# A transformer block on one core: the MLP's first layer by two levels of seven products instead of one

## The chip, the core and the metric

The kernel runs on one core of a Trainium2 chip. Its engines are TensorE (PE: matmuls, and their weight loads PEld), VectorE (DVE), ScalarE (ACT), GpSimd (POOL) and SyncE (SP, which here only starts transfers); each works through its own queue in order, and semaphores tie them together. The metric is device time in microseconds (us) of one execution.

## The reference

The input x has 2 sequences of 2048 tokens with 512 features; all is float32. With D = 512, 16 heads and a hidden width of 2048:

```python
mod = silu(condition) @ Wada + bada
sh_a, sc_a, gt_a, sh_m, sc_m, gt_m = split(mod, 6, axis=1)
xm = layernorm(x, g1, be1) * (1.0 + sc_a[:, None, :]) + sh_a[:, None, :]
x = x + gt_a[:, None, :] * causal_attention(xm, Wqkv, Wproj, bproj)
xm = layernorm(x, g2, be2) * (1.0 + sc_m[:, None, :]) + sh_m[:, None, :]
h = gelu(xm @ W1 + b1)                          # W1: 512 x 2048
x = x + gt_m[:, None, :] * (h @ W2 + b2)        # W2: 2048 x 512
```

## The kernel before

The first two thirds of the time go to modulation, the q, k, v products and the causal attention of the two sequences (`Row(0)`, `Row(1)`), each with its output projection (`project_phase`). The last third, from 1605 us on in the profiled execution, is the MLP. This is where the change is.

**Seven products.** A product of two 2x2 block matrices needs eight block products; with sums of blocks taken first, seven do (Winograd's form of Strassen's method). The code names them A11, S1, S2, S3, S4, A12, A22, and `seven` runs them over three accumulators in PSUM: `ps_a` takes A11, S2, S3 and A22 one on top of the other, `ps_b` takes S1 and S4, `ps_c` takes A12. After each product the accumulator's present value is taken out: `first` keeps it in a spare tile `c`, `last` adds an earlier `c` and yields a quarter of the result. So a later product on the same accumulator must wait until the earlier value has been read. The sums of the weights' blocks are made ahead, in the class `Quarters`, on GpSimd (L913) during the q, k, v stages, and kept in DRAM (`w1d`, `w2d`, L902). The sums of the tokens' blocks are made on VectorE (`difference`, L1239).

**The MLP's loop.** It takes `NM` = 4 pairs of groups of 512 tokens, 1024 tokens at a time. For each pair:

- First layer (`Hidden.block`, L1462, once for each of `HF` = 8 columns of weight blocks): one level of seven products over (two halves of the 512 features) x (two halves of the hidden width) x (two groups of tokens). A product is `HK` = 2 matmuls of 128x128 weights with 512 tokens. ScalarE copies three values out (L1483), VectorE adds (`combine`, L1318), and ScalarE applies the bias and gelu (L1492) as it writes the hidden values `h`.
- Second layer (`Hidden.outer`, L1502, called by `tail`, once for each of the seven outer names): two levels. The outer level splits the hidden width, the output features and the groups of tokens; inside each of its seven, `seven` runs again on halves of those. A product is `C` = 4 matmuls with 256 tokens. The token sums that this needs are a list of tasks in an order written out by hand in `Hidden.__init__`: `inner(n)` gives the four inner sums of the outer name n, `first_sums`, `difference_of` give the outer sums T1 to T4. `hid.pop` runs the next task, normally one after each product; `need` runs tasks at once, in order, until the one that the next product needs is done. Some tasks are already run in the first layer (`among` in the main loop, up to six).

In the second layer of a pair the next pair is normalised and transposed (`normed`, `ln_t`); in the first layer the pair before is transposed back, added to the residual and stored (`rows_out`, after products of the second and third block).

**Order.** Matmuls and the operations wrapped in `act(...)` keep the order of the program on their engine. Weights come in through SP's queue (`load_w1`, `load_w2`) into three rotating tiles `w7`; a load is issued when the tile that it overwrites has been used.

Of the kernel before, what the change touches and what calls it, by code (L numbers as in the profile page):

```python
# [8 lines left out]
F32 = mybir.dt.float32  # L9
F32R = mybir.dt.float32r  # L10
# [17 lines left out]
def dit_block_kernel(  # L28
# [99 lines left out]
    def picks():  # L128
# [56 lines left out]
    w1d = [  # L185
        dram.tile([P, 7, C // 2, P], F32, tag=f"w1d{f}", name=f"w1d{f}")
        for f in range(FC // 2)
    ]
    w2d = [
        dram.tile([P, C, 7, P], F32, tag=f"w2d{n}", name=f"w2d{n}")  # L190
        for n in range(7)
# [38 lines left out]
    def transposed(pool_, psum, xts, n0, mv, rstd, a, c, b, dst, xns=None):  # L230
# [8 lines left out]
        for t, xt in enumerate(xts):  # L239
            if by_act:  # L240
                continue
            xn = pool_.tile([P, D], F32, tag="xn", name="xn", bufs=3)
            n = n0 + t
            nc.vector.tensor_scalar(
                xn, xt, mv[:, n, 0:1], rstd[:, n : n + 1], ALU.subtract, ALU.mult
            )
            xns.append(xn)
# [512 lines left out]
    class Qkv:  # L760
# [41 lines left out]
        def group(self, g, hp, between, among):  # L802
# [6 lines left out]
            for f in range(C):  # L809
                for which in range(2):  # L810
# [8 lines left out]
                    hl = hp.tile([P, 2, MT], F32R, tag="hl", name="hl", bufs=4 - b)  # L819
# [69 lines left out]
    class Quarters:  # L889
# [25 lines left out]
        def step(self):  # L915

            self.store()
            f, self.at = self.at, self.at + 1
            if f >= FC // 2 + C:
                return  # L920
            if not self.rooms:
                self.rooms = self.more_rooms()
            w = self.rooms.pop(0)
            base = ((A11, 0, 0), (A12, 0, 1), (A21, 1, 0), (A22, 1, 1))
            if f < FC // 2:
                w = w[:, :piece].rearrange("p (n c d) -> p n c d", n=7, d=P)
                for n, i, k in base:
                    at = (f + i * FC // 2) * P
                    nc.gpsimd.dma_start(
                        w[:, n],  # L930
                        w1_v[:, k * C // 2 : (k + 1) * C // 2, at : at + P],
                    )
                self.sums(lambda n: w[:, n])
                self.to = [(w1d[f], w)]
                return
            r = f - FC // 2
            w = w.rearrange("p (n k d) -> p n k d", n=7, k=7)
            for n, i, k in base:
                for n2, i2 in ((A11, 0), (A21, 1)):
                    at = (2 * i + i2) * P  # L940
                    k0 = 2 * k * C + r
                    nc.gpsimd.dma_start(
                        w[:, n, n2 : n2 + 3 : 2],
                        w2_v[:, k0 : k0 + C + 1 : C, at : at + P],
                    )
            self.sums(lambda n: w[:, n, A11 : A22 + 1])
            self.sums(lambda n: w[:, :, n])
            self.to = [(w2d[n][:, r], w[:, n]) for n in range(7)]
            self.store()
# [208 lines left out]
    with pool("qkv1") as qp, pool("ps_qkv1", bufs=6, space=PSUM) as ps_mm:  # L1158
# [18 lines left out]
        def also(g, n):  # L1177
            k = NG * g + n // 4
            if n % 4 == 1 and (k < 2 or k % 2 == 0):
                quarters.step()  # L1180

        with pool("hl1") as hp:
            def rooms():

                w = hp.tile([P, 49 * P], F32, tag="w7", name="w7")
                if quarters.at > FC // 2:
                    return [w]
                return [w[:, k * piece : (k + 1) * piece] for k in range(2)]

            quarters.more_rooms = rooms  # L1190
            qkv.run(hp, also)
            assert quarters.at >= FC // 2 + C
            quarters.store()
# [8 lines left out]
    with ExitStack() as mlp:  # L1202
# [4 lines left out]
        OUTER = (A11, S1, A12, S2, S3, A22, S4)  # L1207
        half_t = MT // 2
# [14 lines left out]
        def normed(m, n, xts):  # L1223

            xns = []
            for t, xt in enumerate(xts):
                k = 2 * m * MTT + 2 * n + t
                xn = wp.tile([P, D], F32, tag="xn", name="xn", bufs=3)
# [23 lines left out]
        def load_w1(f):  # L1252
            w = wp.tile([P, C * C * P], F32, tag="w7", name="w7", bufs=3)
            w = w[:, :piece].rearrange("p (n k d) -> p n k d", n=7, k=HK)
            nc.sync.dma_start(w, w1d[f])
            return w

        def load_w2(n, part):
            k = C - part
            w = wp.tile([P, C * C * P], F32, tag="w7", name="w7", bufs=3)  # L1260
            w = w[:, : C * k * P].rearrange("p (r k d) -> p r k d", k=k, d=P)
            nc.sync.dma_start(w, w2d[n][:, :, C * part : C * part + k])
            return w

        loads = []
        for _ in range(NM):
            loads += [lambda f=f: load_w1(f) for f in range(HF)]
            loads += [lambda n=n, k=k: load_w2(n, k) for n in OUTER for k in range(2)]
        w7 = []

        def next_weights():
            if loads:
                w7.append(loads.pop(0)())
# [32 lines left out]
        for _ in range(3):  # L1306
            next_weights()
# [6 lines left out]
        ]  # L1314
        Y = [mp.tile([P, 2, MT], F32, tag=f"y{n}", name=f"y{n}", bufs=1) for n in range(4)]
# [7 lines left out]
        def seven(product, w, first, last, among):  # L1323

            def bank(name):
                return ps_mm.tile([P, MT], F32, tag="mm", name=name)[:, :w]

            a, b = bank("ps_a"), bank("ps_b")
            product(a, A11, True)
            c11 = first(a, 0, 0)
            among(0)
            product(b, S1, True)  # L1340
            c22 = first(b, 1, 1)
            among(1)
            product(a, S2, False)
            c12 = first(a, 0, 1)
            among(2)
            product(b, S4, False)
            last(b, 0, 1, c12)
            among(3)
            product(a, S3, False)
            last(a, 1, 1, c22)  # L1350
            among(4)
            c = bank("ps_c")
            product(c, A12, True)
            last(c, 0, 0, c11)
            among(5)
            product(a, A22, False)
            last(a, 1, 0, None)
            among(6)

        class Hidden:  # L1360
# [3 lines left out]
            def __init__(self):  # L1364
# [7 lines left out]
                self.todo, self.made, self.at = [], set(), 0  # L1372
# [35 lines left out]

                first_sums(0)
                difference_of("T3", b12, b22, b12, 0, (0,))  # L1410
                inner(A11, (1,))
                inner(S1, (1,))
                inner(A11, (2, 3, 4))
                first_sums(1)
                inner(S1, (2, 3, 4))
                inner(A12)
# [45 lines left out]
            def block(self, f, among):  # L1462

                w = w7.pop(0)
# [6 lines left out]
                }  # L1471

                def product(ps, n, new):
                    for k in range(HK):
                        mm(
                            ps, w[:, n, k, :], ops[n][:, k],
                            start=new and k == 0, stop=k == HK - 1,
                            skip_group_check=not new,
                        )

                def first(ps, half, g):
                    c = spare(MT)
                    act(nc.scalar.copy(c, ps))  # L1483
                    return c

                def last(ps, half, g, c):
                    d = self.part(half, g, f)
                    if c is not None:
                        combine(d, c, ps)
                        ps = d  # L1490
                    act(
                        nc.scalar.activation(  # L1492
                            d, ps, AF.Gelu, bias=col(r_b1 + half * HF + f, 1)
                        )
                    )

                seven(product, MT, first, last, among)
                next_weights()

            def outer(self, n, dst, base, among, each=None):  # L1500

                w = []  # L1502
# [12 lines left out]
                def product(ps, k, new):  # L1515
# [4 lines left out]
                    if k in (A11, S3):  # L1520
                        w.append(w7.pop(0))
                    at = k - C * (len(w) - 1)
                    y = ops[k]()
                    for r in range(C):
                        mm(
                            ps, w[-1][:, r, at, :], y[:, r],
# [5 lines left out]
                    if k in (S4, A22):  # L1532
                        next_weights()
# [23 lines left out]
                seven(product, half_t, first, last, among)  # L1557
# [11 lines left out]
        def tail(m, hid, among, each):  # L1569
# [13 lines left out]
            for n, dst, base in (  # L1583
# [9 lines left out]
                def then(k):  # L1593
                    if k in (1, 3) and later:
                        later.pop(0)()
                    hid.pop()
                    among(n, k)
# [45 lines left out]
        ready = False  # L1643
        for m in range(NM):
            hid = Hidden()
            for f in range(HF):

                def among(k):
                    if f >= C and k in (2, 5):
                        if len(hid.made) < 6:  # L1650
                            hid.pop()
                    if ready and f in (1, 2) and k == 6:
                        rows_out(m - 1, f - 1, res, [(0, C)], True)

                hid.block(f, among)
                if ready and f < 2:
                    res = residual(m - 1, f, "xr")
# [81 lines left out]
```

## Time and profile before

| what | value |
|---|---|
| time, median of 3 runs | 2367.77 us (2367.48 to 2368.69) |
| profiled execution: time / span | 2366.88 us / 2365.2 us |
| TensorE clock granted | 1.00 |
| busy: PE, DVE, POOL, ACT | 2336.9, 1397.6, 1079.2, 924.1 us |
| one first layer (pair 0: 1605.21 to 1701.35 us) | 8 blocks x 7 products |
| one second layer (pair 0: 1701.35 to 1789.46 us) | 7 x 7 products and 4 groups of transposes |

The profile's times count from the span's start. A matmul of float32 appears in the records as two instructions: the first layer's 448 matmuls with 512 tokens are 896 rows, the second layer's 784 with 256 tokens are 1568 rows. A row's duration contains the time in the array's pipeline, which overlaps the next matmul; what a product takes of TensorE's time is the distance from its start to the next one's. Operation names are given as output<-inputs, with the tiles' names.

### The profile page before, as it was taken

To read this page: it belongs to the slowest core of one execution; us is meant where nothing else is said; L and a number is where in the kernel's file an instruction comes from. 1 tells how busy PE (TensorE), PEld (TensorE's weight loads), DVE (VectorE), ACT (ScalarE), POOL (GpSimd) and SP (SyncE) were. 2 spreads that over 40 slices of the span, in tenths; PEclk is the share of its full clock that TensorE was granted. 3 is DMA by queue.
4 is the path that set the end of the run, shared out by engine and by line. 5 is a ranking of instruction groups with operands and counts; after the bars stand their busy time and mean duration, and the time that the engine had idled before them with its cause. 6 is when DMAs were issued, how large, how long until landed. Compare 5 with 4: busy or idle time off the path is not lost.

```text
span 2365.2 us, 32348 instructions
## 1 busy us (share of the span) xinstructions
PE 2336.9 (99%) x11469; PEld 1294.6 (55%) x11469; DVE 1397.6 (59%) x2868; ACT 924.1 (39%) x1736; POOL 1079.2 (46%) x1219
## 2 busy tenths in 40 slices
PE   8999999999999999999999999999999999999998
PEld 4455555555544445555555555444585486487477
DVE  3466666767656636576666766553483374365356
ACT  2113555555555012155555555613322332332321
POOL 1052997978793646379887997460000000000000
PEclk9999999999999999999999999999999999999999
DMA  7577215151223788650513214272254254353433
GB/s 258 188 249 195 49 28 118 27 117 46 83 106 132 255 259 259 220 113 24 117 46 85 59 31 144 78 252 100 98 170 146 94 179 139 119 166 132 135 124 129
DMA packets 134106, 311.49 MB, mean 132 GB/s; under 512 B 14208, under 2 KB 29100, under 8 KB 129080
## 3 DMA queue, kind: packets, MB, share of 16 engines
q1 hardware_dynamic: 126096, 277.13, 38.9%
q0 software_dynamic: 7472, 31.75, 3.7%
q8 instruction: 90, 1.47, 0.3%
q14 instruction: 72, 0.59, 0.1%
q10 hardware_dynamic: 376, 0.55, 0.1%
HBM read 229.95 MB, written 87.29 MB: 134 GB/s over the span
## 4 chain that ended last, share of the span: by engine, by line
PE 96%; DVE 2%; POOL 1%; issue 0%; DMA 0%; ACT 0%; SPq 0%; POOLq 0%; ACTq 0%; DVEq 0%
PE st L203 20%; PE ps_a L203 17%; PE o L203 11%; PE s L203 10%; PE ps_qk L203 9%; PE ps_b L203 9%; PE ps_v L203 5%; PE ps_o L203 5%; PE ps_c L203 4%; PE sm L203 4%; PE ps_xt L211 1%; POOL ee L614 1%; PE ps_o L211 1%; DVE mx L461 0%; DVE junk L456 0%
## 5 line engine op out<-in xcount | busy, mean ns | idle before, releaser
L586 ACT ACTIVATE e<-st 128x512 f32<-128x512 f32 (+1 forms) x1152 | 574.6, 578 | 428.1 <-PE st L203 361.6
L614 POOL TENSOR_TENSOR ee<-ee,e 128x512 f32<-128x512 f32 x424 | 529.2, 1289 | 4.4 <-ACT e L586 4.0
L461 DVE TENSOR_REDUCE mx<-s 128x1 f32<-128x512 f32 x604 | 407.9, 688 | 204.5 <-PE s L203 203.1
L203 PE MATMUL s<-kst,qst 128*128 128x512 f32 (+3 forms) x1032 | 463.7, 451 | 5.7 <-DVE mx L461 2.9
L203 PE MATMUL st<-qst,kst 128*128 128x512 f32 (+3 forms) x1280 | 409.4, 387 | 0.0
L203 PE MATMUL ps_a<-sum,w 128*128 128x256 f32 (+1 forms) x1088 | 346.6, 454 | 0.0
L203 PE MATMUL o<-e,vv 128*32 128x512 f32 (+3 forms) x2560 | 300.5, 538 | 2.0 <-POOL e L592 2.0
L456 DVE CUSTOM_DVE_ANT_0 junk<-s,causal 128x512 bf16<-128x512 f32 (+3 forms) x428 | 209.3, 489 | 135.5 <-PE s L203 127.6
L203 PEld LDWEIGHTS s<-kst,qst 128*128 128x128 f32 x1032 | 194.4, 189 | 155.7 <-DVE mx L461 55.6
L203 PEld LDWEIGHTS st<-qst,kst 128*128 128x128 f32 x1280 | 227.3, 188 | 94.2 <-issue 62.2
L203 PEld LDWEIGHTS ps_a<-sum,w 128*128 128x128 f32 x1088 | 206.3, 190 | 109.8 <-issue 91.4
L614 POOL TENSOR_TENSOR ee<-e 128x512 f32<-128x512 f32 x168 | 210.4, 1285 | 101.4 <-ACT e L586 101.0
L203 PE MATMUL ps_qk<-xmT,wqkv 128*128 128x512 f32 x512 | 239.0, 594 | 1.8 <-DVE xmT L263 1.8
L592 POOL TENSOR_SCALAR_AFFINE_SELECT e<-e 128x128 f32<-128x128 f32 (+1 forms) x384 | 122.4, 357 | 135.0 <-ACT e L586 132.3
L203 PE MATMUL st<-fold,sel 32*128 32x512 f32 (+1 forms) x1152 | 149.1, 481 | 0.9 <-ACT vv L843 0.5
L203 PEld LDWEIGHTS ps_qk<-xmT,wqkv 128*128 128x128 f32 x512 | 93.9, 190 | 97.0 <-issue 90.4
L1318 DVE TENSOR_TENSOR h<-c,ps_b 128x512 f32<-128x512 f32 x32 | 22.0, 687 | 202.4 <-PE ps_b L203 202.4
L203 PEld LDWEIGHTS st<-fold,sel 32*128 32x128 f32 x1152 | 59.3, 181 | 144.8 <-ACT e L586 86.6
L203 PE MATMUL ps_v<-wqkv,xmT 128*128 128x512 f32 x256 | 122.3, 594 | 0.0
L203 PE MATMUL ps_b<-sum,w 128*128 128x256 f32 (+1 forms) x384 | 120.6, 450 | 0.0
L203 PEld LDWEIGHTS o<-e,vv 128*32 128x32 f32 x2560 | 61.1, 108 | 102.0 <-issue 81.0
L1492 ACT ACTIVATE h<-h,cols 128x512 f32<-128x512 f32 x96 | 69.2, 721 | 118.6 <-DVE h L1318 118.6
(155 smaller groups left out, 2601.3 us busy)
## 6 DMA issues: line engine op xcount, KB each, us to landing
qst<-q SPq DMA_DIRECT2D x128, 256.0 KB
w<-w1d SPq DMA_DIRECT2D x32, 896.0 KB
w<-w2d SPq DMA_DIRECT2D x28, 1024.0 KB
kst<-k SPq DMA_DIRECT2D x24, 1024.0 KB
w<-w2d SPq DMA_DIRECT2D x28, 768.0 KB
q<-hl SPq DMA_DIRECT2D x32, 512.0 KB
k<-hl SPq DMA_DIRECT2D x32, 512.0 KB
w2d<-w POOLq DMA_DIRECT2D x28, 448.0 KB, 6.5
```

The costliest lines, as they stand in the source:

```text
L203: return tc.keep_in_program_order(nc.tensor.matmul(*args, **kw))
L211: return tc.keep_in_program_order(nc.tensor.transpose(dst, src, ident[:n, :n]))
L456: nc.vector.tensor_tensor_reduce(junk[:, :w], s[:, :w], causal[:, QB - w :], 1.0, MASKED, ALU.add, ALU.max, m,)
L461: nc.vector.tensor_reduce(m, s[:, :w], axis=AX.X, op=ALU.max)
L586: act(nc.scalar.activation(e[:, :w], sts[h][:, :w], AF.Exp))
L592: nc.gpsimd.affine_select(d, d, pattern=[[0, len(tiles)], [1, P]], compare_op=ALU.is_ge, fill=0.0, base=0, channel_multiplier=-1,)
L614: act(engine.tensor_tensor(dst, x, y, ALU.add))
L1318: act(nc.vector.tensor_tensor(dst, x, y, ALU.add))
L1492: nc.scalar.activation(d, ps, AF.Gelu, bias=col(r_b1 + half * HF + f, 1))
```

## The change

The first layer goes to two levels as well: `first_layer` takes the place of `block`. The outer level is the same split as before; inside each of its seven steps (`one_outer`) the seven products run again, over halves of (256 features) x (1024 hidden columns) x (512 tokens). A product is 4 matmuls of 128x128 weights with 256 tokens, and each accumulator is two PSUM banks (a pair of 128-column blocks in each). Each step gives a quarter matrix of hidden values; since the outer level has to add these too, they stay in the tiles of `h`, and the outer sums are made there in place: in each step after the first two, an earlier matrix (`base`) is added to the values taken out, on VectorE, or, for two of them, on GpSimd after ScalarE's copy; two further sums (`adds`, four operations each) follow the steps S2 and S3. Gelu becomes a pass of its own, in place, from a list `later`, two operations after each product. After the first step the inner order begins with S1 rather than A11.

`Quarters` now makes only the outer sums of both weights. The inner sums are made in the MLP's first pair by GpSimd (`Weights.add`: four operations a step, one after each product from the fourth on) in the tile that holds the step's weights, and stored from there to DRAM (`w1e`, `w2e`); the later pairs load them ready. The weights of a step (14 KB a partition) have one of two rooms.

The order of the tasks in `Hidden` changes (`inner(A11)` comes first, T3's first half later), and four rather than six tasks are run ahead in the first layer. Outside the MLP, `transposed` normalises in place (`xn = xt`), and the tile `hl` has four buffers in the second sequence instead of three.

```diff
-            xn = pool_.tile([P, D], F32, tag="xn", name="xn", bufs=3)
+            xn = xt
...
-                    hl = hp.tile([P, 2, MT], F32R, tag="hl", name="hl", bufs=4 - b)
+                    hl = hp.tile([P, 2, MT], F32R, tag="hl", name="hl", bufs=4)
...
+        class Weights:
+            def load(self, at, part):
...
+                m, layer, n = order[at]
+                room = rooms[at % 2]
+                if m:
+                    k = slice(0, 3) if part == 0 else slice(3, 7)
+                    nc.sync.dma_start(room[:, k], (w1e if layer == 1 else w2e)[n][:, k])
+                elif part:
+                    src = (w1d if layer == 1 else w2d)[:, n]
+                    nc.sync.dma_start(
+                        room[:, 2:6], src.rearrange("p k (i f) d -> p (k i) (f d)", i=2)
+                    )
+                    self.adding.append((at, 0))
+            def add(self):
...
+                    nc.gpsimd.tensor_tensor(
+                        room[:, slot[d]], room[:, slot[x]], room[:, slot[y]], op
+                    )
...
+                if step < 3:
+                    self.adding.insert(0, (at, step + 1))
+                else:
+                    nc.gpsimd.dma_start((w1e if layer == 1 else w2e)[n], room)
+            def used(self, k):
+                if k == 2:
+                    self.load(self.at + 2, 0)
+                elif k == 6:
+                    self.load(self.at + 2, 1)
+                if k >= 3:
+                    while self.adding and self.adding[0][0] == self.at + 1:
+                        before = len(self.adding)
+                        self.add()
+                        if k < 6 or len(self.adding) < before:
+                            break
...
+            if lead == A11:
+                a = bank("ps_a")
+                c11 = one(a, A11, 0, True, 0, 0, False)
+                b = bank("ps_b")
+                c22 = one(b, S1, 1, True, 1, 1, False)
+            else:
+                b = bank("ps_b")
+                c22 = one(b, S1, 0, True, 1, 1, False)
+                a = bank("ps_a")
+                c11 = one(a, A11, 1, True, 0, 0, False)
+            c12 = one(a, S2, 2, False, 0, 1, False)
+            one(b, S4, 3, False, 0, 1, c12)
+            one(a, S3, 4, False, 1, 1, c22)
             c = bank("ps_c")
+            one(c, A12, 5, True, 0, 0, c11)
+            one(a, A22, 6, False, 1, 0)
...
+                inner(A11)
                 first_sums(0)
-                difference_of("T3", b12, b22, b12, 0, (0,))
-                inner(A11, (1,))
                 inner(S1, (1,))
-                inner(A11, (2, 3, 4))
                 first_sums(1)
                 inner(S1, (2, 3, 4))
+                difference_of("T3", b12, b22, b12, 0, (0,))
                 inner(A12)
...
+                    def first(ps, i, t):
+                        cs = []
+                        for pair in range(2):
+                            c = spare(MT).rearrange("p (r t) -> p r t", r=2)
+                            if base is None:
+                                act(nc.scalar.copy(c, ps[pair]))
+                            elif (i, t) == (0, 1):
+                                combine(c, piece_of(base, i, t, pair), ps[pair])
+                            else:
+                                act(nc.scalar.copy(c, ps[pair]))
+                                act(
+                                    nc.gpsimd.tensor_tensor(
+                                        c, c, piece_of(base, i, t, pair), ALU.add
+                                    )
+                                )
+                            cs.append(c)
+                        return cs
...
+                    def then(k):
+                        self.gelu()
+                        for _ in range(2):
+                            if adds:
+                                adds.pop(0)()
+                        if todo and todo[0][0] <= at + 1:
+                            inner_x()
+                        elif at >= 5 and len(self.made) < 4:
+                            self.pop()
+                        among(at, k)
...
+                for at, (n, dst, base) in enumerate((
+                    (A11, u, None),
+                    (S1, c22, None),
+                    (A12, c11, u),
+                    (S2, u, u),
+                    (S3, u, u),
+                    (S4, c12, c12),
+                    (A22, u, u),
+                )):
+                    one_outer(at, n, dst, base)
+                    if n in (S2, S3):
+                        d = c12 if n == S2 else c22
+                        for i in range(2):
+                            for pair in range(2):
+                                adds.append(
+                                    lambda d=d, i=i, pair=pair: combine(
+                                        rows4(*d, i, pair), rows4(*u, i, pair),
+                                        rows4(*c22, i, pair),
+                                    )
+                                )
```

## The prediction

> **What bounds the kernel now.** I read the page's busy line and its 40 slices first.
>
> ```profile
> PE 2336.9 (99%) x11469; PEld 1294.6 (55%) x11469; DVE 1397.6 (59%) x2868; ACT 924.1 (39%) x1736; POOL 1079.2 (46%) x1219
> PE   8999999999999999999999999999999999999998
> PEclk9999999999999999999999999999999999999999
> DVE  3466666767656636576666766553483374365356
> POOL 1052997978793646379887997460000000000000
> ```
>
> TensorE is the bound everywhere, at full clock. The MLP is the last 13 slices: POOL is idle there, DVE 30 to 80% busy. So fewer matmuls are time won, one for one, until another engine makes TensorE wait; the question is only where that happens. TensorE's timeline gives the products' pitch in both layers (columns: start, us, engine, line, operation, output<-inputs, count).
>
> ```profile
> 1605.21 1.88 PE L203 MATMUL ps_a<-xm,w 128*128 128x512 f32 x4
> 1606.93 1.88 PE L203 MATMUL ps_b<-sum,w 128*128 128x512 f32 x4
> ...
> 1699.63 1.88 PE L203 MATMUL ps_a<-sum,w 128*128 128x512 f32 x4
> 1701.35 1.89 PE L203 MATMUL ps_a<-h,w 128*128 128x256 f32 x8
> 1703.07 1.89 PE L203 MATMUL ps_b<-sum,w 128*128 128x256 f32 x8
> ...
> 1789.46 1.88 PE L203 MATMUL ps_a<-xm,w 128*128 128x512 f32 x4
> ```
>
> First layer of pair 0: 1605.21 to 1701.35, 56 products, 96.15/56 = 1.717 us each. A second-layer product, four matmuls with 256 tokens, is what the first layer will now have: 1701.35 to 1789.46 less 3.5 for groups of transposes gives 84.6/49 = 1.727 us. ScalarE's timeline shows when a result can be read, VectorE's what its sums cost.
>
> ```profile
> 1791.37 0.59 ACT L1483 COPY c<-ps_a 128x512 f32<-128x512 f32 x1 [0.45 <-PE ps_a L203]
> ```
>
> The product begun at 1789.46 hands over at 1791.17 and is read at 1791.37: 0.20 us after the next begins.
>
> ```profile
> 1765.48 0.42 DVE L1318 TENSOR_TENSOR y<-y,ps_a 128x256 f32<-128x256 f32 x1 [0.17 <-PE ps_a L203]
> 1765.82 1.22 DVE L1239 TENSOR_TENSOR sum<-h 128x1024 f32<-128x1024 f32 x1
> 1766.96 1.22 DVE L1318 TENSOR_TENSOR y<-y,y 128x1024 f32<-128x1024 f32 x1
> 1768.10 0.41 DVE L1318 TENSOR_TENSOR c<-y,ps_a 128x256 f32<-128x256 f32 x1
> ```
>
> A sum of 1024 elements takes 1.14 us from start to start, one of 256 about 0.34; 512 elements out of PSUM 0.69 (0.64 apart, by the group h<-c,ps_b). While these run, POOL is idle. What DVE and POOL do to each other shows only in the attention, on both timelines:
>
> ```profile
> 725.69 3.58 DVE L614 TENSOR_TENSOR ee<-e 128x512 f32<-128x512 f32 x4
> ...
> 725.86 1.67 POOL L434 TENSOR_TENSOR kst<-kst,bgate 128x512 f32<-128x512 f32 x1 [16.81 <-DVE bgate L424]
> ```
>
> Four DVE sums take 2.48 us in a row elsewhere (at 729.91), here 3.58: during one POOL sum, DVE lost 1.10 us. By the answer for source line 614, such a DVE sum takes 682 ns in the median and 1766 at most. [...]
>
> **The matmuls.** A pair's first layer goes from 56 x 1.717 to 49 x 1.727 us: 96.15 to 84.6, so 11.5 saved, four pairs: **-46.1**. [...]
>
> In what follows a step is one of the seven outer ones (7 x 1.727 = 12.1 us), S its start.
>
> **Starts.** The first inner sums of a layer now need two sums in a row on VectorE, behind the last results of the second layer, or in pair 0 behind the normalising. Pair 0: five sums of 0.34 are 1.7, with 0.06 to resume, 1.8; later pairs some 0.5, as A11's token sums go behind two evictions. **+3.3** (0 to 8).
>
> **Gelu.** A product fills its accumulator's two banks one after the other, so a half can be read while the other is made: S1's halves at S + 1.06 and 1.93 (0.86 and 1.73, and 0.20). In step S2 ScalarE's queue holds S1's copies, the first two gelus, then A11's copies: 1.93 + 0.59 = 2.52, gelus (0.70 apart, L1492) to 3.92, A11's first copy to 4.51, and the S2 product on the same bank at 4.57 rather than 3.45: 1.1 a pair, and one table load of 1.28 (the row of ACT_TABLE_LOAD): **+5.7** (0 to 12). Behind it on ScalarE wait only further copies. Gelus of later steps lie in the shadow of the next term.
>
> **Adds against POOL.** After steps S2 and S3, DVE gets four adds of 1.14 in the first two products of the next step, and two inner sums of 0.34, from S + 0.9, when the last results are out. Alone these end at 6.1. The S3 product, due at 6.9, needs ps_a's S2 value read, which stands behind them: 6.1 + 0.64 + 0.06 = 6.8, no wait. But in the same stretch POOL has its four adds on `c` (ready behind ScalarE's copies of S1 and A11 at 1.65, 2.5, 3.4 and 4.3), and each costs DVE 1.1: 10.3 rather than 6.1, and S3's product runs at 11.0, 4.1 late. Behind DVE's eviction wait the accumulator, and TensorE's whole queue. Eight such steps at 4.2 are 33.6, with about 3 more in pair 0, where POOL also sums weights: **+36.6**. Bounds: nothing (the two dodge each other), and 8 x 4 x 1.77 = 57 if every POOL add costs DVE a full blocked row. I take near one loss per POOL add, as the row above has it.
>
> **Step A22.** Before it DVE has, in S4, four adds, four inner sums, about ten evictions and three second-layer tasks, more than 12.1 us. What is left over makes A11's and S3's products wait some 1.6 each: 4 x 1.6 = **+6.4** (0 to 13).
>
> **Second layer.** Only four tasks are ahead instead of six, so the fourth sums of S2 and A22 are run by `need` behind the S1 product of their own step; before, they were done a step earlier. Each is 1.22 on DVE plus what stands ahead of it: S2's product waits 1.75, A22's 2.4, 4.1 a pair: **+16.4** (0 to 25; 0 if DVE runs ahead).
>
> **Weights in pair 0.** POOL's four sums a step block second-layer tasks as above: **+4** (0 to 10). The transfers I take as hidden. A room turns round in two steps, 24.2 us: load 5.3 + sums 5.1 + store 9.2 (1792 KB by the row below, 4.6 per 896 KB) = 19.6.
>
> ```profile
> w1d<-w POOLq DMA_DIRECT2D x8, 896.0 KB, 4.6
> ```
>
> Load and store are 2.88 MB in 12.1 us, 238 GB/s; the slices reach 259. By the slow row of that view (wqkv through POOL's queue, 1024 KB in 11.6) it would be 11.6 + 5.1 + 20.3 = 37, up to 6.4 late a step, and 90 us over 14 steps. That is the range's far end; I take the near row, the same kind of store to DRAM.
>
> **Nothing for.** `xn` in place: x's buffer comes free after TensorE's transposes instead of DVE, covered by the five projections (some 17 us) before it is reloaded; a full miss would cost one load of 256 KB. `hl` with four buffers and the smaller `Quarters` lie under the q, k, v matmuls, where the POOL slices leave gaps; +-3. Rows_out loses DVE room: +0.3.
>
> **Sum.** 3.3 + 5.7 + 36.6 + 6.4 + 16.4 + 4 = 72.4 lost, 46.1 won: +26.3. The profiled execution of 2366.9 becomes 2393.2; the median of the runs was 0.9 above that execution: **2394**.
>
> **The rivals.** *The other side, the adds dodge:* DVE and POOL run beside each other, or POOL's adds fall into DVE's gaps. The two terms on blocking (36.6 and 4) go, the others stay at 31.8, and the time is 2367.8 - 14.3 = 2353. For it: POOL's adds are only 5 of a step's 12.1 us, and DVE's evictions out of PSUM leave holes. Against it: the 1.10 us above, and that adds and `c` are both released in the first half of a step. It decides where blocking costs under 14.3 us, 1.8 at each of the eight steps. *Pair 0 short of weights:* the slow DMA row holds in part; +26 (up to +90) on the forecast, 2420. For it, POOL's queue carries 1.8 MB a step, ahead of which it must finish its sums; against it, the row of 4.6. *Only the matmuls count:* all waits hidden by slack, 2321; against it, TensorE has now only 12.1 us a step and DVE more than that in S4. *No change:* the terms balance within 5 us.
>
> **How the numbers follow.** Forecast 0.60, the adds dodge 0.22 (2340 to 2362), weights late 0.10, matmuls alone 0.04, no change 0.04. A measurement here tells 0.2%, 4.7 us, from nothing. The forecast's low edge and the balance give 0.07 within it; 0.25 below, 0.68 above. The likeliest's own range is 2378 to 2412 (term four between 20 and 55); to hold 8 in 10 it must take in most of the dodge case and some of the late weights: 2350 to 2416.
>
> **What would show it.** First-layer products at 1.727 where nothing waits; TensorE idle before the S3 product of steps S3 and S4, about 4 us each, released by DVE on ps_a; DVE's 1024-element adds at 2.2 rather than 1.2 us while POOL works; waits of 1.7 to 2.4 on the task sums in the second layer's S2 and A22; in pair 0, no waits on `w`. Wrong if those adds keep 1.2 us (then the dodge), or if TensorE's long waits are on a DMA or POOL and end with pair 0 (late weights).

## The result, and the profile after

The changed kernel takes 2405.47 us (median of 4 runs, 2401.53 to 2407.41) against 2367.62 for the kernel before in the same comparison: ratio 1.0157, interval 1.0139 to 1.0175. The profiled execution took 2403.96 us with a span of 2402.2, 37.0 more than before.

The page of the kernel after: busy line, and the slices of the four engines and the clock.

```profile
PE 2320.7 (97%) x12141; PEld 1433.0 (60%) x12141; DVE 1632.3 (68%) x3164; ACT 937.1 (39%) x1784; POOL 1264.5 (53%) x1349
PE   8999999999999999999999999998899899899998
DVE  3466666766757536667666666657896876877787
POOL 1062898978774561089787979356662400310310
PEclk9999999999999999999999999999899999999999
```

TensorE is busy 16 us less and the kernel is 37 us longer. In the MLP, from slice 27 on, POOL is no longer idle, and TensorE has holes in the slices of three of the four first layers (the 8s in slices 28, 29, 32 and 35; in the fourth the slices stay at 90% or more). The waits of TensorE within the MLP name the holes (columns: waiter, releaser, us in total, times, longest; the five largest lines):

```profile
PE ps_a L201 <- DVE c L1360: 34.6, 10, 4.9
PE ps_a L201 <- ACT c L1585: 6.8, 8, 2.2
PE ps_o L209 <- DVE xr L1360: 3.7, 9, 0.5
PE ps_a L201 <- DVE h L1360: 2.7, 1, 2.7
PE ps_b L201 <- ACT c L1581: 1.8, 1, 1.8
```

33.1 us of the first line are eight waits before the S3 product of steps S3 and S4: 4.90 twice in pair 0 and 3.88 or 3.89 six times in the later pairs. One of them, in pair 2, on the timelines of VectorE, POOL and TensorE:

```profile
2063.67 0.69 DVE L1360 TENSOR_TENSOR h<-h,ps_a 128x512 f32<-128x512 f32 x1 [0.17 <-PE ps_a L201]
2064.28 3.43 DVE L1360 TENSOR_TENSOR h<-h,h 128x1024 f32<-128x1024 f32 x2
2067.63 1.48 DVE L1223 TENSOR_TENSOR sum<-xm 128x256 f32<-128x256 f32 x1
2069.04 4.49 DVE L1360 TENSOR_TENSOR h<-h,h 128x1024 f32<-128x1024 f32 x2
...
2073.78 1.27 DVE L1360 TENSOR_TENSOR c<-h,ps_a 128x512 f32<-128x512 f32 x2
```
```profile
2065.25 7.19 POOL L1587 TENSOR_TENSOR c<-c,h 128x512 f32<-128x512 f32 x4 [7.99 <-ACT c L1585]
```
```profile
2068.73 1.89 PE L201 MATMUL ps_b<-sum,room 128*128 128x256 f32 x8
2074.51 3.68 PE L201 MATMUL ps_a<-sum,room 128*128 128x256 f32 x8 [3.89 <-DVE c L1360]
2078.03 1.89 PE L201 MATMUL ps_c<-sum,room 128*128 128x256 f32 x8
```

The four adds (`h<-h,h`) take 3.43 and 4.49 us, where a pair of them is 2.3 alone. An inner sum that took 0.34 apart takes 1.48. POOL's four adds take 7.19 where one alone is 1.26. The reading of S2's value (`c<-h,ps_a`) stands behind all that, and TensorE waits 3.89. VectorE is not waiting for POOL's results in this stretch: its rows follow one another without a gap, they are longer. The third fence shows something that the prediction did not have: the product after the wait took 3.52 us to the start of the next, twice its 1.73. The granted clock was 0.50 there (stretch, length, PE busy, clock, DMA share, GB/s; in the wait, behind it, and after that):

```profile
2071.00:2074.50 3.50, 0.00 (x0) 1.00 0.33 139
2074.62:2078.02 3.40, 3.40 (x8) 0.50 0.00 0
2078.03:2081.44 3.41, 3.41 (x17) 1.00 0.02 5
```

Added up over the span (TensorE's timeline by pair): 46.1 won on products; 45.7 more idle in the first layers, 2.2 in the second; 29.2 on products that were slower than 1.727; and the MLP began 6.1 later (1611.31 instead of 1605.21). That is 37.1. Of the 29.2, 22.2 were lost by the products right behind the ten waits of more than 2 us, all at a clock of 0.50 as above; most of the rest is a product's last 0.16 us, which no next one covers when a wait follows (1.89 instead of 1.73), and 0.1 on the first product behind a short wait.

### The profile page after: what moved, and what is told of

Its sections match the earlier page's. It is cut to its first block, busy times and chain, and to the rows that moved or that the text cites. A ratio compares the mean times of both kernels' runs of the same rounds, so it can differ in the third digit from the quotient of the medians.

```text
span 2402.2 us, 34530 instructions
## 1 busy us (share of the span) xinstructions
PE 2320.7 (97%) x12141; PEld 1433.0 (60%) x12141; DVE 1632.3 (68%) x3164; ACT 937.1 (39%) x1784; POOL 1264.5 (53%) x1349
## 5 line engine op out<-in xcount | busy, mean ns | idle before, releaser
L201 PE MATMUL ps_a<-sum,room 128*128 128x256 f32 x1504 | 371.3, 392 | 44.9 <-DVE c L1360 34.6
L201 PEld LDWEIGHTS ps_a<-sum,room 128*128 128x128 f32 x1504 | 288.9, 195 | 98.0 <-DVE c L1360 36.8
L1587 POOL TENSOR_TENSOR c<-c,h 128x512 f32<-128x512 f32 x80 | 125.0, 1590 | 422.2 <-DVE sum L1223 279.9
L201 PE MATMUL ps_b<-sum,room 128*128 128x256 f32 x608 | 145.3, 382 | 2.6 <-ACT c L1581 1.8
L201 PEld LDWEIGHTS ps_b<-sum,room 128*128 128x128 f32 x608 | 115.9, 192 | 20.0 <-issue 2.2
```

What stands on the lines that cost most here:

```text
L201: return tc.keep_in_program_order(nc.tensor.matmul(*args, **kw))
L1587: nc.gpsimd.tensor_tensor(c, c, piece_of(base, i, t, pair), ALU.add)
```

## The experiments

Theory 1: POOL's adds on `c` and VectorE's sums without an operand in PSUM take turns (a pair of them took 3.43 and 4.49 us above, 2.3 alone), and this makes the long waits; the slow products follow from the waits. Rivals: VectorE is too full anyway; or the new form of the layer itself runs slower.

**POOL's adds taken away.** In `first`, the add on GpSimd goes:

```diff
                             else:
                                 act(nc.scalar.copy(c, ps[pair]))
-                                act(
-                                    nc.gpsimd.tensor_tensor(
-                                        c, c, piece_of(base, i, t, pair), ALU.add
-                                    )
-                                )
```

> Leaves out the sum with `base` for the values of S1 and A11 in every step (the copies on ScalarE stay), so POOL has no adds in the first layer except the weights' sums of pair 0. Theory 1, the two engines take turns: the 1024-element adds go back to 1.2 us, the S3 product of steps S3 and S4 no longer waits (33 us of idle go), and the slow products that follow such waits go with them (17 us in pairs 1 to 3, some more in pair 0): 2345 to 2358. Rival, VectorE is too full whatever POOL does: the waits stay at 2 to 4 us each, 2390 to 2405. Rival on the clock, the slow products come from the new form of the layer and not from the waits: they stay when the waits go, 2372.

2350.8 us, ratio to before 0.9933 (0.9916 to 0.995), so 55 us less than with them. The groups of VectorE's adds in the MLP, first after, then without POOL's adds (count | busy, mean ns | idle before):

```profile
L1360 DVE TENSOR_TENSOR h<-h,h 128x1024 f32<-128x1024 f32 x32 | 63.3, 2019 | 0.0
```
```profile
L1360 DVE TENSOR_TENSOR h<-h,h 128x1024 f32<-128x1024 f32 x32 | 37.7, 1219 | 0.0
```

The same 32 adds went from 2019 ns to 1219, and no wait on VectorE at S3 is left; the three largest lines of waits in its MLP:

```profile
PE ps_a L201 <- ACT c L1585: 7.0, 8, 2.1
PE ps_o L209 <- DVE xr L1360: 3.7, 9, 0.5
PE ps_b L201 <- ACT c L1581: 1.8, 1, 1.8
```

The first layers of pairs 1 to 3 fell from 104.2 to 105.5 us to 92.57, and of what their products took beyond 1.727 each (5.1 to 6.4 us) 1.2 was left. Theory 1 stands in what the runs show: VectorE's sums are longer while POOL adds, and the waits come from that; whether the two take turns, the runs do not show. The slow products come from the waits and not from the form of the layer.

**Two of the four adds moved behind the reading of S2.**

```diff
-                        for _ in range(2):
+                        for _ in range(2 if k in (0, 2) else 0):
                             if adds:
                                 adds.pop(0)()
```

> The four adds after S2 and S3 come after the products 0 and 2 of the next step rather than 0 and 1, so that the value of S2 is read before the second two. Theory 1: S3's product waits 1.4 us instead of 3.9, A22's 1.3; with no wait over 2 us the products after them run at their pitch: 2370 to 2385. Rival, VectorE is too full: what is moved comes back as a wait on A22 of 3 us or more, 2395 to 2410.

2383.9 us, ratio 1.0064 (1.0049 to 1.0079). In pairs 1 to 3 the S3 products of the two steps now wait 0.55 and 0.77 and their A22 products 1.61, and the products lose 2.3 us a pair beyond their pitch instead of 5 to 6. In pair 0 the rival's sign appears: waits of 4.85 and 3.81 before A22. POOL has the weights' sums there too; whether they are the cause was not tried in this order. The order alone is worth 22 us.

**Normalising in place, alone, in the kernel before.**

```diff
-            xn = pool_.tile([P, D], F32, tag="xn", name="xn", bufs=3)
+            xn = xt
```

> The kernel before with nothing changed but `xn = xt` (normalising in place). Theory: in place the buffers of x come free later, the next loads and normalisations come later and stand ahead of the maxima, and this is the 6 us that the kernel after lost ahead of the MLP: 2371 to 2375. Rival: those 6 us come from the other edits there (the sums of the weights, `hl` with four buffers): 2367 to 2369.

2372.15 us against 2368.85, ratio 1.0016 (1.0006 to 1.0025): 3.3 us, with an interval of 1.4 to 5.9, of the 6.1 that the MLP began later. In its profiled execution the MLP began at 1610.74, 5.5 later than in the kernel before, and the longest wait that is new is this (TensorE, then VectorE):

```profile
1440.95 0.33 PE L211 MATMUL ps_m<-ident,mhl 128*128 128x128 f32 x1 [2.97 <-DVE mx L461]
```
```profile
1439.75 0.55 DVE L244 TENSOR_SCALAR qst<-qst,mv,rstd 128x512 f32<-128x512 f32 x1 [3.68 <-DMA sum<-sums]
1440.21 0.69 DVE L461 TENSOR_REDUCE mx<-s 128x1 f32<-128x512 f32 x1
```

VectorE sat 3.68 us at a normalisation whose operand had not come, with the attention's maxima queued behind it. The operand's load is not late: it was issued at 1430.69, in the kernel before at 1430.58. What moved is the normalisation. In the kernel before the first of these four ran 100 us later (the two loads, this run and before, then VectorE before):

```profile
1430.69 4.46 SPq L412 DMA_DIRECT2D qst<-x1d  x4
```
```profile
1430.58 4.17 SPq L412 DMA_DIRECT2D qst<-x1d  x4
```
```profile
1541.28 0.62 DVE L244 TENSOR_SCALAR xn<-qst,mv,rstd 128x512 f32<-128x512 f32 x1
```

So in place it stands right behind its load in VectorE's queue, ahead of the maxima. That it can, since it has no buffer `xn` of its own to wait for, is a reading and was not tried by itself. In the kernel after, the same place shows 1.73 us of waiting. A second one there, 2.86 behind four normalisations of `x` in a row (2.87 us at 910.00), is not in this run, so the rest of the 6.1 stays open. In the eight profiles of the kernel after and of its variants in this section, the MLP began 3.5 to 7.2 us later than before.

**Pair 0 without weights' sums.** Every load takes the form of the later pairs, from `w1d`/`w2d`, and nothing is added to `adding`:

```diff
-                if m:
+                if m or True:
                     k = slice(0, 3) if part == 0 else slice(3, 7)
-                    nc.sync.dma_start(room[:, k], (w1e if layer == 1 else w2e)[n][:, k])
+                    src = (w1d if layer == 1 else w2d)[:, n]
+                    src = src.rearrange("p k (i f) d -> p (k i) (f d)", i=2)
+                    nc.sync.dma_start(room[:, k], src[:, slice(0, 3) if part == 0 else slice(0, 4)])
```

> The kernel after with pair 0 loading seven ready blocks like the later pairs (they, and the other pairs', are blocks of the outer sums, so the weights' inner sums and their stores are left out). Theory: the sums on POOL are what pair 0 has over the other pairs: its first layer takes 100 to 102 us instead of 113.3 and its second 88.1 instead of 91.4, 2388 to 2393. Rival: pair 0 is slow because of its start and the transfers, 2400 to 2406.

2392.95 us, ratio 1.0105 (1.009 to 1.012): 12.5 less than after. The first layer of pair 0 took 104.9 us (113.3 after; 100 to 102 expected), its second 88.11 (91.36). The weights' sums and their stores cost 12 us. The waits that went, and the two at S3 that shrank by 1.0 each, were on VectorE, so POOL's adds are the likely way; that was not tried apart from the transfers, which changed in this run too. What pair 0's first layer still has over the others is its start (1.78), the wait with the table load (2.06) and slow products. TensorE has no wait on a load of `room` in any run: the loads and stores were hidden.

**The adds spread out.** The adds after S2 in pieces of 512 (`at_k` is the product that a piece follows), each before its piece of `u` is overwritten; those after S3 one after each of products 2 to 5:

```diff
-                            if adds:
-                                adds.pop(0)()
+                        while adds and adds[0][0] <= k:
+                            adds.pop(0)[1]()
...
+                        if n == S2:
+                            for at_k, i, t in ((0, 1, 1), (2, 0, 1), (4, 0, 0), (5, 1, 0)):
...
+                        else:
...
+                                        2 + 2 * i + pair,
```

> All of the change kept; the adds after S2 are cut into halves of 512 and done piece by piece in step S3, each before the piece of `u` that it reads is overwritten (two at its start, the others after products 2, 4 and 5); those after S3 are done one at a time after products 2 to 5 of step S4. Theory 1: few of them now meet a POOL add, S3's product waits under 0.3 us, A22's 0.5 to 1, and no wait in pairs 1 to 3 is long enough to slow the products after it: 3 to 5 us a pair less than with the adds after products 0 and 2, and 8 to 12 in pair 0: 2355 to 2368. Rival, VectorE is too full in these steps (12.8 us of work in 12.1): the waits only move, 2375 to 2390.

2391.02 us, ratio 1.0093 (1.0078 to 1.0108): a miss, 1 us above the rival's range. In pairs 1 to 3 the S3 products of steps S3 and S4 no longer wait, as expected, and step S3's A22 waits 0.33; but step S4's A22 waits 1.75, and in step A22 a new wait of 3.53 stands before the S3 product. The adds that were moved late pushed the four second-layer tasks into step A22, beside its POOL adds. Pair 0 keeps waits of 2.44 and 4.05. So VectorE's load over these steps does matter, not one step's order alone.

**Gelu behind A11's copies**, on top of that: `self.gelu()` only where `k` is not 0.

> The same as e5_spread, and no gelu after the first product of a step, so that the copies of A11's value on ScalarE come ahead of the gelus. Theory: the two waits of 0.65 us a pair on ScalarE's copy go, and most of the 2.2 in pair 0: 5 to 7 us less than e5_spread, 2349 to 2362. Rival: the gelus end later and the second layer's first sums wait for h: no gain, or up to 3 us more.

2381.24 us, ratio 1.0058 (1.0041 to 1.0075), 9.8 less than without (5 to 7 expected; the range missed because it started from a lower e5_spread). The waits of 0.65 on ScalarE are gone, and pair 0's of 2.15. Part of it came back: the wait in step A22 grew from 3.53 to 4.36, which is set by VectorE.

**The tasks after POOL's adds.** To test that the meeting in step A22 is the cause, the second-layer tasks are held until POOL is done there, and S4's adds are placed around its evictions. Both go in at once (against the run before):

```diff
-                                        2 + 2 * i + pair,
+                                        (0, 2, 5, 6)[2 * i + pair],
...
-                        elif at >= 5 and len(self.made) < 4:
+                        elif at == 6 and k >= 3 and len(self.made) < 4:
```

> As e6_spread_gelu, but the four second-layer tasks run only in step A22 after products 3 to 6, when POOL is done with its adds on `c`, and of the four adds in step S4 one comes after each of the products 0, 2, 5 and 6. Theory 1: the 4.4 us wait of step A22, where tasks and left-over adds met POOL's adds, goes, and with it the slow products behind it; S4's A22 product waits 0.7 instead of 1.75: 2355 to 2365. Rival, VectorE is too full over the steps S3 to A22 taken together: the tasks are then missing at the start of the second layer, with waits of 2 to 4 us there, 2372 to 2385.

2365.07 us, ratio 0.9987 (0.9978 to 0.9996). In pairs 1 to 3 the wait of 4.36 is gone, and the second layers have no wait; S4's A22 still waits 1.58, not 0.7. Pair 0 is worse: 8.69 before the S3 product of step S4 and 4.35 in the second layer. The 8.69 shows the meeting at its plainest (VectorE, then POOL): two adds of 512, 1.29 apart from POOL, take 10.04, until POOL's adds on `c` and the weights' sums, one behind the other, are done.

```profile
1682.76 10.04 DVE L1360 TENSOR_TENSOR h<-h,h 128x512 f32<-128x512 f32 x2
```
```profile
1681.98 4.94 POOL L1587 TENSOR_TENSOR c<-c,h 128x512 f32<-128x512 f32 x4
1686.89 5.36 POOL L1282 TENSOR_TENSOR room<-room 128x512 f32<-128x512 f32 x4
```

The same with S4's adds after products 0, 4, 5 and 6:

> As e8_tasks_late, with S4's adds after products 0, 4, 5 and 6, so that three of them follow the reading of S3's value. Theory 1: no wait in S4, but one or two adds spill into step A22 and meet POOL's adds on `c` there, 0 to 1.5 us a pair: 2352 to 2365. Rival, VectorE too full: as in e8_tasks_late, 2372 to 2385.

2361.05 us (2359.14 to 2366.79), ratio 0.9975 (0.9963 to 0.9986): this one beats both kernels, the one before by 7 us. The five largest lines of waits in its MLP:

```profile
PE ps_a L201 <- DVE h L1360: 9.1, 9, 2.7
PE ps_a L201 <- DVE y L1360: 4.1, 3, 2.7
PE ps_o L209 <- DVE xr L1360: 3.7, 9, 0.5
PE ps_b L201 <- ACT c L1581: 1.8, 1, 1.8
PE ps_a L201 <- DVE c L1360: 1.6, 2, 1.4
```

The first layers of pairs 1 to 3 take 92.32 us each, against 101.09 before and 104.2 or more after: 26 us won there. Pair 0 gives 9 back (96.9 and 96.4 for its two layers, against 96.1 and 88.1), and the MLP began 7.3 later than before in this profile. The same operations as in the kernel after, in another order and with the adds after S2 cut into pieces, are 44 us faster.

## Why the prediction was right, and where not

The time came 11.5 us above the point and inside the range, which is 66 us wide. Step by step:

- **The matmuls, -46.1: right.** Where nothing waits, a first-layer product takes 1.727 us (second layers 84.6 for 49; first layers 84.6 plus waits, slow products and transposes). A product of half-width matmuls cost what the row of the second layer said.
- **Adds against POOL, +36.6: right in cause, place and size.** The eight waits sum to 33.1 (33.6 forecast; by the prediction's own terms 6.1 + 4 x 1.10 is 10.5, not 10.3). The 3 more for pair 0 came as 2.7 in another place, before the A22 product of step A12 (`<- DVE h`); it went with the weights' sums, as did 1.0 of each of pair 0's two waits of 4.90. Taking POOL's adds away removed them all. The adds `h<-h,h` took 2019 ns with POOL's adds and 1219 without; the evictions, which read one operand from PSUM, took 0.69 in both. In the kernel after, one of these ran within POOL's four adds and a second began there; both took 0.69, and POOL's four 5.01, 1.25 each (VectorE, then POOL):

```profile
2055.97 0.69 DVE L1360 TENSOR_TENSOR c<-h,ps_a 128x512 f32<-128x512 f32 x1 [3.83 <-PE ps_a L201]
2056.83 0.69 DVE L1360 TENSOR_TENSOR c<-h,ps_a 128x512 f32<-128x512 f32 x1 [0.17 <-PE ps_a L201]
```
```profile
2052.26 5.01 POOL L1587 TENSOR_TENSOR c<-c,h 128x512 f32<-128x512 f32 x4 [9.92 <-ACT c L1585]
```

  That each POOL add costs VectorE one 1.10 held for these eight, not in general: see the 10.04 us above.
- **Second layer, +16.4: wrong.** It measured 2.2 of idle, all in pair 0, and none there without the weights' sums. The failed step is "the fourth sums of S2 and A22 are run by `need` behind the S1 product of their own step ... S2's product waits 1.75". `need` only sets where a sum stands in VectorE's queue; TensorE waits for the tile that it reads. S2's product reads the second sum, and the fourth is read by A22's product, four products later. Step S2 of pair 1, TensorE and VectorE:

```profile
1960.79 1.89 PE L201 MATMUL ps_b<-sum,room 128*128 128x256 f32 x8
1962.52 1.89 PE L201 MATMUL ps_a<-sum,room 128*128 128x256 f32 x8
```
```profile
1961.33 1.22 DVE L1223 TENSOR_TENSOR sum<-h,h 128x1024 f32<-128x1024 f32 x1
1963.06 1.22 DVE L1223 TENSOR_TENSOR sum<-h,sum 128x1024 f32<-128x1024 f32 x1
```

  S2's product starts at 1962.52, on time, and the fourth sum begins after it.
- **Step A22, +6.4: wrong in place.** It has one wait of 0.65 to 0.75 a pair, on ScalarE's copy behind gelu, not on VectorE. (Two products at 1.6 in four pairs would have been 12.8; the sum took one.) **Gelu, +5.7:** step S2 has 2.16 in pair 0 and 0.65 in the others, 4.1. The two together are the 6.8 of ScalarE's line, against 12.1.
- **Starts, +3.3:** 1.79 and three times 0.26, 2.6. **Weights, +4:** too small. 12 us went when the sums were taken away: 2.7 in step A12, 2.0 at S3, 2.2 in the second layer, the rest mostly slower products behind such waits. That the transfers are hidden held.
- **Ahead of the MLP, "nothing" +-3: wrong.** It was +6.1. The step "xn in place ... covered by the five projections" looked at the matmuls that hide the load and not at VectorE's queue, in which a normalisation now stands in front of the attention's maxima and waits for its load. This accounts for some 3.3 of the 6.1; the rest is open.
- **Missing: the slow products.** 29.2 us, in no term and no rival, most of it at half clock.

So the sum of waits was 25 too high (72.4 against 47.9) and two costs of 35 in all were missing; that the point was near is luck, because these nearly cancel. The loss itself came from what was missing: the measured waits alone (47.9) only balance the 46.1 won. The rival in which the adds dodge fell: they met in every one of the eight steps.

## What to carry over

Where two engines slow each other down, as VectorE and POOL do here (2019 ns for an add of 1219, 7.19 us for POOL's four of 1.26), work that is off TensorE's chain still sets its time: place such operations so that they do not meet, and look at each engine's whole queue between a result and its reader, not at busy shares (here 68% and 53%). An instruction's place in a queue and what a reader waits for are two things; price a wait by the tile that is read. A win of 2% on matmuls (46 us) was lost to a handful of waits; reordering alone brought 44 us back, which left 7 of the 46.

## What was not expected of the hardware

A long wait of TensorE cost more than itself here. In the first and second layers of the profiles of the kernel after and its variants, after the 131 waits of 0.2 to 1.8 us the next products lost at most 0.3 us (beyond 1.727 each, without the 0.16 ahead of a next wait); after each of the 28 waits of 3.5 us and more they lost 1.6 to 3.2 us further; of the 15 between 2.06 and 2.74, ten cost 1.8 to 1.9 and five at most 0.3. The slowest products took 3.57 us, double the 1.73, and the granted clock shows it, at 0.50 behind a wait in the rows above and in the means of the kernel after (from, to; length, PE busy, clock, DMA share, GB/s; the first two lines are pair 0, the third is the first layer of pair 1):

```profile
1611.31:1724.61 113.30, 96.09 (x393) 0.91 0.49 186
1724.61:1815.97 91.36, 89.12 (x425) 1.00 0.70 256
1815.97:1920.18 104.21, 94.01 (x425) 0.97 0.51 170
```

What sets the difference among the 15 between 2.06 and 2.74 was not tried. So, as an estimate from these numbers, a wait that is cut from 3.9 us to 1.6 is worth about 4 us, not 2.3.
